# A two-layer graph kernel: three dense chunks of layer 0 in place of four

## The chip, the core and the metric

The kernel runs on one core of a Trainium2 chip, in float32. The metric is the device time of one execution in microseconds. A core has TensorE (PE; PEld is its weight load), VectorE (DVE), ScalarE (ACT), GpSimd (POOL) and SyncE (SP), each with its own instruction stream in order, and 16 DMA engines which serve the transfers that SP, ACT and POOL issue.

## What is computed

```python
x, adj                      # (8, 2048, 128), (2048, 2048); adj = R is sparse, about 0.4%
def L0(inputs, relation):   # layer 0
    sj, si = inputs @ w_j, inputs @ w_i
    res = si[:, :, None] + sj[:, None, :] + relation[None] * w_r + g_b
    return jnp.einsum('bij,bjd->bid', res, inputs) @ weight + bias
def L1(X, A1, A2):          # layer 1, called with A1 = A2 = adj
    x1 = einsum('bnf,nw->bwf', X, A);  x2 = 2 * einsum('bnf,nw->bwf', x1, A) - X
    return relu(concat(X, x1, x2, x1, x2) @ Theta1 + bias)
x = layernorm(x + L0(x, adj))
x = layernorm(x + L1(x, adj, adj))
```

So layer 0 is R times Y, with Y = x times (w_r weight), and terms of rank one; layer 1 is two products with R transposed ("hops").

## The kernel before, in words

The 2048 nodes are 16 chunks of 128. A tile `Y[c]` holds 128 nodes x 8 batches x 128 features (512 KB). R is sparse, so most chunks of output are not computed with all of R: for each chunk the kernel makes seven lists of at most 128 rows each (four lists of 32 output columns, two of 64, one of 128; "tile", "half" and "chunk" lists), gathers those rows of Y from DRAM with seven indirect DMAs of 512 KB, gathers the weights of R that belong to them, and multiplies the gathered rows by small blocks of weights (`listed_rows`), with the diagonal block apart (`own_rows`).

The stages, in the order of the program:

1. *Load stage* (`mask_rows`, `y_chunk`, in one loop over the chunks). R is loaded by rows, each chunk is reduced to a mask of its non-zero tiles of 32 on VectorE, transposed on TensorE, and, if the chunk will be computed by lists, its transpose is stored in the DRAM tensor `rr_d[c]` (L292). x is loaded, and Y made of it. The transposes of the first three chunks (`NA = 3`) stay in SBUF (`first_at`, in `wide[0]` to `wide[2]`), and chunk 0 of layer 0 is summed here already (L342).
2. *Dense stage* (the loop over `c in range(ND)`, `ND = 4`). Chunks 0 to 3 of layer 0 are made with all of R: pass c sums chunk c + 1 over 16 values of j, two products of 128 x 128 by 128 x 512 each (L845). The transposes of chunk 3 are made in the pass before it, from a second load of R (`ar2`, `transpose_group`). Between the products of chosen j stand the steps that make the lists: `tile_ranks`, `tile_lists`, `tile_lists_end`, `half_ranks`, `chunk_ranks`, `candidates` (all with TensorE and VectorE) and eight times `list_round` (VectorE alone: L562 finds the eight largest, L564 takes them out). Here SyncE also issues `copy_r` (R's columns, copied in DRAM to the second half of `rr_d`, L414), `more_rows` (nine more rows of each `rr_d`, L600) and the stores of Y to `y0_d` (L798). GpSimd issues the gathers of weights (`gathers`), each held back until the product of the j before it is done.
3. *List stage of layer 0*: twelve chunks in the order `seq` (9 to 14, 4 to 8, 15). `put(c)` issues what is left of a chunk's weight gathers and calls `keep_r`, by which VectorE masks the gathered weights; `fetch_lists` issues the seven gathers of Y into a ring of nine tiles (`G`, that is `Y[0]` to `Y[8]`); `listed_rows` multiplies (L886); `finish0` adds x and normalizes; `make_u` transposes the result (X1^T, kept in `x1t[c]`) and stores U = X1 times Theta.
4. *First hop* and *second hop* over all 16 chunks with lists, gathering rows of U and of the first hop's result. The four dense chunks' X1^T come back from the DRAM tensor `xt_d`; those of the twelve others have stayed in SBUF (`x1t`).

Weight gathers are a list of jobs `(c, q, n)`: q true for the four tile lists of chunk c, false for the other three. A job of a listed chunk fetches 128 rows of 1 KB from `rr_d` (weights for layer 0 and layer 1 together), one of a dense chunk rows of 512 bytes from R itself. Four slots of `stage` take a chunk's set; at most three sets wait for `keep_r`:

```python
jobs = [(c, q, n) for cs in (seq, range(ND)) for q in (True, False) for c in cs
        for n in range(4 if q else 3)]
...
            if n == 0:
                if len(waiting) == 3:
                    keep_r(*waiting.pop(0))
```

The framework adds the waits between engines and to some extent orders independent instructions; `keep_in_program_order` holds marked ones in the order of the program on their engine, `behind` puts one instruction after another by hand. On every engine and queue the resulting order is fixed when the kernel is built. "Issue" of a DMA by SP, ACT or POOL means that the instruction occupies that stream until it is sent.

Of the kernel before, what the change touches and what calls it, by code (L numbers as in the profile page):

```python
# [18 lines left out]
def kernel(  # L19
# [42 lines left out]
    ND = 4  # L62
# [222 lines left out]
    NA = 3  # L285
# [11 lines left out]
    def mask_rows(n, c):  # L297
# [9 lines left out]
        if c < NA:  # L307
            first_at[c] = transpose_rows(c, a, False, by_chunk(wide[c]))
# [39 lines left out]

    chunks = list(range(NA)) + list(range(ND, NC)) + list(range(NA, ND))
    for n, c in enumerate(chunks):  # L350
        mask_rows(n, c)
        if n == NA - 1:
            xw = wide[3].rearrange("p (n b f) -> p n b f", n=2, b=B)
            xslot += [xw[:, 0], xw[:, 1]]
# [100 lines left out]
    cand = by_chunk(wide[1])  # L455
# [175 lines left out]
    def chunk_lists_end():  # L631
# [6 lines left out]
        nc.tensor.matmul(pn, ones[:, 0:1], miss, start=True, stop=True)  # L638
        nc.vector.tensor_reduce(miss[0:1, 0:1], pn, AX.X, ALU.max)
        return nc.vector.tensor_scalar(  # L640
# [28 lines left out]
    def keep_r(c, q, m, st):  # L669
# [16 lines left out]
    jobs = [  # L686
        (c, q, n) for cs in (seq, range(ND)) for q in (True, False) for c in cs
        for n in range(4 if q else 3)
    ]
# [56 lines left out]
    for n in range(4):  # L746
        pair = wide[n].rearrange("p (n b f) -> p n b f", n=2, b=B)
        spare += [pair[:, 0], pair[:, 1]]
    spare += Y[NG4 + 3:]
# [3 lines left out]
    free = [rc2[:, 4 * N - n * BD:4 * N - (n - 1) * BD].rearrange("p (b f) -> p b f", b=B)  # L753
            for n in range(1, 3)]
    held = {(0, c): Y[c] for c in seq if c >= NG4}
    held |= {(1, c): t for c, t in zip(seq[-2:], free)}
    held |= {(2, c): t for c, t in zip(hops[-7:], [own_t[4], free[0]] + [
# [27 lines left out]
    with nc.allow_non_contiguous_dma(reason="512-byte rows of blocks"):  # L785
        pending, accs, xr = None, acc0, load_x(0, "xr", nc.sync)
        at1, ar2 = first_at[1], None
        for c in range(ND):
            if c + 1 < ND:
                if NA <= c + 2 < ND:  # L790
                    ar2 = load_rows(c + 2, wide[3])
                xr1 = load_x(c + 1, "xr", nc.sync)
            if c < 2:
                copy_r(2 + 5 * c, 7 + 5 * c)
            if 1 <= c <= 2:
                for n in range(8 * c - 8, 8 * c):
                    tc.keep_in_program_order(
                        nc.sync.dma_start(out=y0_d[n * P:(n + 1) * P, :], in_=flat(Y[n]))  # L798
                    )
            if c == 0:  # L800
                make_ub()
                more_rows()
                rank1(0, accs, si_t(0))
            else:
                z = finish0(c, accs, xr, c > 2)
# [277 lines left out]
```

## Time and profile before

| | |
|---|---|
| median of 3 runs | 846.56 us (841.54 to 848.09) |
| the profiled execution | 877.11 us, its span 875.3 us |
| busy, share of the span | PE 89%, PEld 45%, DVE 41%, ACT 20%, POOL 48% |
| DMA | 264.28 MB, mean 302 GB/s |
| load stage, about | 0 to 147 us |
| dense stage, about | 147 to 302 us |
| list stage of layer 0, about | 302 to 475 us |
| first hop, about | 475 to 690 us |
| second hop, about | 690 to 875 us |

The profile is of one execution. A line of the groups gives source line, engine, operation, output and input names with buffer numbers left out, shapes, count, then busy time, the mean of one in ns, and the idle time of the engine just before with what ended it. A line of the timeline gives start and duration in microseconds, engine, source line, operation, names and count, and in brackets the idle time before it with its releaser. Where a releaser is "issue", the profile shows nothing that the engine waited for; "remote" is a releaser that it can't name. Both the DRAM tensors y0_d and y_d appear as y_d. SPq and the like are the queues by which an engine issues DMAs.

### The profile page before, as it was taken

Reading aid. Unit: us, or ns where it says so; the run is one execution under the profiler, and the core shown is the slowest. Engines: PE = TensorE matmul, PEld = TensorE weight load, DVE = VectorE, ACT = ScalarE, POOL = GpSimd, SP = SyncE. Lnnn points to the kernel's source line nnn. Section 1 sums busy time; section 2 is a strip of 40 time slices with the busy share of each in tenths; the row PEclk is TensorE's granted clock in tenths of the full one; section 3 lists DMA queues with packets and bytes.
Section 4 is the critical chain, followed back from the end, with each engine's and each line's share of the span. In section 5 each row is a group of like instructions: output and inputs, shape, how many; then the busy total and the mean of one; then the engine's idle time right before and its main releaser. Section 6 shows DMA issues by size and latency. Waiting matters only on the chain.

```text
span 875.3 us, 10807 instructions
## 1 busy us (share of the span) xinstructions
PE 780.9 (89%) x3631; PEld 393.3 (45%) x3631; DVE 360.5 (41%) x1056; ACT 176.1 (20%) x429; POOL 421.2 (48%) x431
## 2 busy tenths in 40 slices
PE   5999988999997799878986899888999999999994
PEld 4666664455443443333334433333433444545441
DVE  5555665344972364435353000000100045556656
ACT  3655653001111222121212000000000001111111
POOL 0000000015676376766666366666655646666660
PEclk9999999899998699999998899999999999999998
DMA  8699999895383899999997699998999889999994
GB/s 276 205 303 301 276 292 278 237 338 223 88 344 99 310 328 313 335 350 354 338 367 259 236 319 364 311 342 321 377 385 358 286 298 369 352 347 345 346 335 170
DMA packets 172283, 264.28 MB, mean 302 GB/s; under 512 B 17458, under 2 KB 123226, under 8 KB 170044
## 3 DMA queue, kind: packets, MB, share of 16 engines
q0 software_dynamic: 49280, 147.41, 47.4%
q1 hardware_dynamic: 99610, 88.37, 31.7%
q10 hardware_dynamic: 23330, 27.73, 8.8%
q8 instruction: 31, 0.51, 0.2%
q14 instruction: 32, 0.26, 0.1%
HBM read 242.03 MB, written 60.96 MB: 346 GB/s over the span
## 4 chain that ended last, share of the span: by engine, by line
PE 56%; DMA 21%; issue 10%; DVE 5%; ACT 3%; POOL 2%; another core or an unknown queue 2%; SPq 0%; POOLq 0%; DVEq 0%; ACTq 0%
PE acc L886 22%; DMA Y<-y_d,idx 10%; DMA Y<-u_d,idx 7%; PE acc L870 7%; PE acc L944 5%; PE acc L845 4%; PE acc L342 3%; PE acc L332 3%; PE pp L403 2%; POOL Y L647 2%; DVE rc L562 2%; PE pt_a L184 1%; DMA rr_d<-rct 1%; DMA rc<-in_adj_dram 1%
## 5 line engine op out<-in xcount | busy, mean ns | idle before, releaser
L647 POOL DMA_INDIRECT Y<-y_d,idx x196 | 194.8, 994 | 126.3 <-PE acc L886 69.3
L886 PE MATMUL acc<-Y,rc 128*32 128x512 f32 (+2 forms) x896 | 226.4, 610 | 19.6 <-issue 9.7
L647 POOL DMA_INDIRECT stage<-rr_d,idx x84 | 85.5, 1018 | 227.2 <-PE acc L845 200.3
L647 POOL DMA_INDIRECT Y<-u_d,idx x112 | 111.3, 994 | 67.4 <-PE acc L886 35.6
L886 PEld LDWEIGHTS acc<-Y,rc 128*32 128x32 f32 (+2 forms) x896 | 60.9, 128 | 174.9 <-issue 115.8
L886 PE MATMUL acc<-Y,rct 128*32 128x512 f32 (+2 forms) x336 | 96.6, 605 | 19.8 <-issue 10.7
L845 PE MATMUL acc<-Y,wide 128*128 128x512 f32 x192 | 86.9, 602 | 0.5 <-issue 0.5
L870 PE MATMUL acc<-Y,rd 128*128 128x512 f32 x140 | 69.0, 615 | 1.1 <-issue 1.1
L886 PEld LDWEIGHTS acc<-Y,rct 128*32 128x32 f32 (+2 forms) x336 | 23.9, 127 | 83.6 <-issue 58.2
L176 DVE COPY z<-acc 128x512 f32<-128x512 f32 x9 | 6.2, 692 | 122.2 <-PE acc L870 42.9
L845 PEld LDWEIGHTS acc<-Y,wide 128*128 128x128 f32 x192 | 35.9, 194 | 39.9 <-issue 39.9
L219 ACT ACTIVATE st<-st,epst 128x8 f32<-128x8 f32 x32 | 10.0, 311 | 213.9 <-DVE st L220 76.9
L384 DVE TENSOR_TENSOR xs<-acc,xs 128x512 f32<-128x512 f32 x24 | 16.4, 683 | 84.0 <-PE acc L886 50.7
L303 DVE TENSOR_REDUCE rc<-rc 128x64 f32<-128x2048 f32 x16 | 36.5, 2282 | 15.5 <-DMA rc<-in_adj_dram 15.5
L184 PE MATMUL pt_a<-ident,rc 128*128 128x128 f32 x240 | 35.2, 282 | 8.0 <-DMA rc<-in_adj_dram 6.0
L332 PE MATMUL acc<-wx,tr_x 128*128 128x130 f32 x256 | 37.4, 290 | 3.9 <-ACT tr_x L178 3.1
L964 DVE SCALAR_TENSOR_TENSOR z<-z,pt_r 128x512 f32<-128x512 f32 x32 | 20.5, 684 | 47.8 <-PE acc L886 21.3
L332 PEld LDWEIGHTS acc<-wx,tr_x 128*128 128x128 f32 x256 | 33.7, 199 | 14.0 <-ACT tr_x L178 6.4
L342 PE MATMUL acc<-Y,wide 128*128 128x512 f32 x64 | 36.1, 646 | 2.5 <-ACT si L340 1.8
L944 PEld LDWEIGHTS acc<-th,wide 128*128 128x128 f32 x256 | 32.5, 196 | 11.5 <-issue 11.3
L184 PEld LDWEIGHTS pt_a<-ident,rc 128*128 128x128 f32 x240 | 28.8, 145 | 17.6 <-issue 14.3
L944 PE MATMUL acc<-th,wide 128*128 128x128 f32 x256 | 32.7, 280 | 4.1 <-issue 4.1
(210 smaller groups left out, 907.3 us busy)
## 6 DMA issues: line engine op xcount, KB each, us to landing
rc<-in_adj_dram SPq DMA_DIRECT2D x16, 1024.0 KB
rr_d<-rct SPq DMA_DIRECT2D x12, 1024.0 KB
rr_d<-in_adj_dram SPq DMA_DIRECT2D x12, 1024.0 KB
xs<-in_x_dram SPq DMA_DIRECT2D x20, 512.0 KB
y_d<-Y SPq DMA_DIRECT2D x16, 512.0 KB
out_dram<-z ACTq DMA_DIRECT2D x16, 512.0 KB
u_d<-u ACTq DMA_DIRECT2D x14, 512.0 KB
Y<-y_d SPq DMA_DIRECT2D x14, 512.0 KB
```

The lines of the kernel that those rows point to most:

```text
L184: mm = nc.tensor.transpose(pt[:, i, :], s, ident)
L303: nc.vector.tensor_reduce(mk[:, c, :], a.rearrange("p (w f) -> p w f", f=TW), AX.X, ALU.max, apply_absolute_value=True,)
L332: nc.tensor.matmul(py[:, i, 0:D + 2], xt[b // HB][:, (b + i) % HB, :], wx, start=True, stop=True,)
L342: nc.tensor.matmul(acc0[h], first_at[0][:, c, :], Y[c][:, h * HB:(h + 1) * HB, :], start=(c == 0), stop=False, skip_group_check=True,)
L403: mm = nc.tensor.matmul(pp[:, i, :], xt[:, h * HB + i, :], th[:, 0, :], start=True, stop=True)
L562: tc.keep_in_program_order(nc.vector.max(top, part))
L647: g = nc.gpsimd.indirect_dma_start(out=out, out_offset=None, in_=src, in_offset=bass.IndirectOffsetOnAxis(ap=ids[:, n:n + 1], axis=0), bou ...
L845: mm = nc.tensor.matmul(accs1[h], at1[:, j, :], Y[j][:, h * HB:(h + 1) * HB, :], start=(j == 0), stop=False, skip_group_check=True,)
L870: in_order(nc.tensor.matmul(accs[h], r, t[:, h * HB:(h + 1) * HB, :], start=start, stop=stop, skip_group_check=True,))
L886: in_order(nc.tensor.matmul(accs[h][w * t:w * t + w], r[:, o + w * t:o + w * t + w], gs[t][:, h * HB * D:(h + 1) * HB * D], start=False, s ...
L944: in_order(nc.tensor.matmul(accs[h][:, b, :], x1t[c][:, h * HB + b, :], th[:, i, :], start=(b == 0), stop=False, skip_group_check=True,))
L964: nc.vector.scalar_tensor_tensor(z[:, hs, :], z[:, hs, :], 0.0, pt, op0=ALU.max, op1=ALU.add)
```

## The change

`ND` is 3 in place of 4. Chunk 3 goes through the lists like the others: in the load stage its transposes are made and stored with those of the rest, in the list stage it is a thirteenth chunk, and its X1^T stays in SBUF. The dense stage has two passes in place of three. The steps that make the lists stand at other j: `tile_ranks` before the first pass, the tile, half and chunk lists' ranks and the candidates in the first pass, the first two rounds of `list_round` at its end, and the other six in the first half of the second pass. The pass's products from j = 8 on are put behind the last step of the lists (`made`). SyncE issues all eleven remaining copies of R in one row and then, after `more_rows`, all sixteen stores of Y. The weight gathers start at j = 4 and take another order: ten tile sets, and then tile and other sets mixed; 47 stand in the dense stage (58 before).

```diff
-    ND = 4
+    ND = 3
@@ load stage @@
-    NA = 3
-        if c < NA:
+        if c < ND:
             first_at[c] = transpose_rows(c, a, False, by_chunk(wide[c]))
-    chunks = list(range(NA)) + list(range(ND, NC)) + list(range(NA, ND))
-    for n, c in enumerate(chunks):
-        mask_rows(n, c)
-        if n == NA - 1:
+    for n in range(NC):
+        mask_rows(n, n)
+        if n == ND - 1:
@@ lists @@
-    cand = by_chunk(wide[1])
+    cand = by_chunk(wide[3])
-        nc.tensor.matmul(pn, ones[:, 0:1], miss, start=True, stop=True)
+        made = nc.tensor.matmul(pn, ones[:, 0:1], miss, start=True, stop=True)
-    jobs = [
-        (c, q, n) for cs in (seq, range(ND)) for q in (True, False) for c in cs
-        for n in range(4 if q else 3)
-    ]
+    sets = [(c, True) for c in seq[:10]]
+    for n, c in enumerate(seq):
+        sets.append((c, False))
+        if n in (0, 4, 7):
+            sets.append((seq[10 + (0, 4, 7).index(n)], True))
+    sets += [(c, q) for q in (True, False) for c in range(ND)]
+    jobs = [(c, q, n) for c, q in sets for n in range(4 if q else 3)]
@@ places of X1^T and of U @@
-    spare += Y[NG4 + 3:]
+    spare += Y[NG4 + 3:LAST] + [free[0], Y[LAST]]
-    held |= {(1, c): t for c, t in zip(seq[-2:], free)}
-    held |= {(2, c): t for c, t in zip(hops[-7:], [own_t[4], free[0]] + [
+    held[1, LAST] = free[1]
+    held |= {(2, c): t for c, t in zip(hops[-7:], own_t[ND:] + [
@@ dense stage @@
-        at1, ar2 = first_at[1], None
-                if NA <= c + 2 < ND:
-                    ar2 = load_rows(c + 2, wide[3])
-            if c < 2:
-                copy_r(2 + 5 * c, 7 + 5 * c)
-            if 1 <= c <= 2:
-                for n in range(8 * c - 8, 8 * c):
-                    (store of Y[n] to y0_d)
             if c == 0:
+                copy_r(2, NC - ND)
+                tile_ranks()
                 make_ub()
                 more_rows()
                 rank1(0, accs, si_t(0))
             else:
-                z = finish0(c, accs, xr, c > 2)
+                z = finish0(c, accs, xr, c > 1)
+            if c == 1:
+                for n in range(NC):
+                    (store of Y[n] to y0_d)
                 for j in range(NC):
                     if c == 0:
-                        if j == 4:  tile_ranks()
-                        if j == 7:  tile_lists()
-                        if j == 10: at = tile_lists_end(); half_ranks()
-                        if j == 14: chunk_ranks(); z = finish0(c, accs, xr, False); layernorm(z, "0_0", at)
-                    if c == 1 and j < 2: candidates(2 * j); candidates(2 * j + 1)
-                    if c == 1 and (j > 1 and j % 2 == 0 or j == NC - 1):
-                        list_round(j // 2 - (j < NC - 1))
-                    if c == 2:
-                        if j == 6: at = chunk_lists_end(); layernorm(z1, "0_1", at)
-                        if j == 9: layernorm(z, "0_2", at)
-                        if j == 8: fetch_own(0, y0_d, seq[0]); late0 = fetch_block(0, seq[0])
-                    if (c > 0 or j > 11) and not (c == 2 and j > 11):
-                        gathers(1 if j % 4 == 3 else 2, mm)
-                    if c == 2 and j > 11: fetch_lists(0, y0_d, seq[0], 2 * j - 22)
-                    if ar2 is not None and j % 2 == 0 and j >= 8: (transpose_group)
+                        if j == 0:  tile_lists(); z = finish0(c, accs, xr, False)
+                        if j == 3:  at = tile_lists_end(); half_ranks()
+                        if j == 6:  chunk_ranks()
+                        if j in (8, 9): candidates(2 * j - 16); candidates(2 * j - 15)
+                        if j == 10 or j == 13: list_round(j // 13)
+                        if j == 11: layernorm(z, "0_0", at)
+                    else:
+                        if j < 8 and j % 3 < 2: list_round(2 + j // 3 * 2 + j % 3)
+                        if j == 8: made, at = chunk_lists_end(); layernorm(z, "0_1", at)
+                                   fetch_own(0, y0_d, seq[0]); late0 = fetch_block(0, seq[0])
+                    if (c > 0 or j > 3) and not (c == 1 and j > 12):
+                        gathers(3 if c == 1 and j == 12 else 1 if j % 4 == 3 else 2, mm)
+                    if c == 1 and j > 12: fetch_lists(0, y0_d, seq[0], 2 * j - 24)
                     for h in range(2):
                         mm = nc.tensor.matmul(accs1[h], at1[:, j, :], Y[j][...], ...)
+                        if c == 1 and j == 8: behind(mm, made)
                 rank1(c + 1, accs1, sit)
-                if c == 1: gathers(2, mm)
-                if c == 2: fetch_lists(0, y0_d, seq[1], NG4 - 7)
+                if c == 0: gathers(2, mm)
+                else: fetch_lists(0, y0_d, seq[0], 7); fetch_lists(0, y0_d, seq[1], NG4 - 7)
             if pending is not None:
-                make_u(*pending)
+                make_u(*pending, tie=in_order)
@@ hops @@
-                if i == 1 and c == 0:
+                if i == 1 and n == NC - 5:
                     while waiting: keep_r(*waiting.pop(0))
```

In this diff some statements of a branch are drawn together on one line. `in_order` puts TensorE's products one behind the other; it stands ahead of the dense stage now.

## The prediction

> **What bounds the kernel now.** I read the busy shares first, then the chain that ended last, then the groups, then GpSimd's timeline, and last those of SyncE, VectorE and TensorE in the dense stage. TensorE is busy 89% and leads the chain, but its share averages over stages, so I looked for the engine that sets the pace in each.
>
> ```profile
> L647 POOL DMA_INDIRECT Y<-y_d,idx x196 | 194.8, 994 | 126.3 <-PE acc L886 69.3
> L647 POOL DMA_INDIRECT stage<-rr_d,idx x84 | 85.5, 1018 | 227.2 <-PE acc L845 200.3
> L647 POOL DMA_INDIRECT stage<-in_adj_dram,idr x28 | 28.1, 1003 | 12.9 <-issue 8.3 <-DMA Y<-y_d,idx 4.3 <-DMA stage<-in_adj_dram,idr 0.3
> ```
>
> GpSimd issues 420 gathers: these 308 and 112 of U (L647). Its own timeline, one chunk of layer 0:
>
> ```profile
> 347.49 0.99 POOL L647 DMA_INDIRECT Y<-y_d,idx  x1 [2.04 <-PE acc L886]
> 348.78 0.99 POOL L647 DMA_INDIRECT Y<-y_d,idx  x1 [0.31 <-issue]
> ...
> 353.97 1.10 POOL L647 DMA_INDIRECT stage<-rr_d,idx  x1 [0.30 <-issue]
> ...
> 359.29 0.99 POOL L647 DMA_INDIRECT Y<-y_d,idx  x1 [0.30 <-issue]
> 362.28 0.99 POOL L647 DMA_INDIRECT Y<-y_d,idx  x1 [1.99 <-remote]
> ```
>
> Ten gathers, 1.30 us from start to start, then 2 us until TensorE frees a buffer: 362.28 - 347.49 = 14.8 us. Steps with nine gathers (first hop, 523.2 to 536.3) take 13.2 us, steps with seven (602.1 to 612.5) 10.4. The difference is 1.3 us a gather, of Y or of a 64 or 128 KB list of R alike: from 302 us on, the number of gathers is the clock. The dense stage before it (147 to 302) is TensorE's, and ends badly:
>
> ```profile
> 273.35 1.98 PE L375 MATMUL acc<-ub,sit 9*128 9x512 f32 x4
> ...
> 286.61 0.69 DVE L384 TENSOR_TENSOR xr<-acc,xr 128x512 f32<-128x512 f32 x1 [9.97 <-remote]
> ...
> 290.24 2.08 PE L403 MATMUL pp<-th,xt 128*128 128x128 f32 x8 [9.14 <-issue]
> ...
> 304.39 0.99 POOL L647 DMA_INDIRECT Y<-y_d,idx  x1 [12.47 <-PE acc L886]
> ```
>
> The last dense chunk is summed at 275.3; VectorE then sits for 9.97 us on something the profile calls "remote", TensorE for 9.14, GpSimd for 12.47.
>
> **What the skill says.** "Perfetto Trace Analysis", DMA Instruction: for a DMA from GpSimd the profiled end is the end of writing descriptors, not of moving data. The trace agrees: 0.99 us each, while the chain has 6 to 7.5 us for such a gather to land. So 1.30 us is a price of issue, the same for small and large ones. "DMA: Bandwidth & Descriptors", Queues, rings and completion order: on each DMA engine the transfers of one issuing queue are taken up in order; so rows sent behind eleven copies wait for them. Agrees in kind: SyncE is held 3.1 us per copy (15.51 for five). "TensorE: Matmul & The Clock Gate", Part 1: after an idle window of about 3.4 us the clock halves. The windows view agrees: granted 0.50 from 280 to 295. "Runtime: NRT & Kernel Launch", Instruction fetch mechanics: engines stream their instructions through a DMA queue, mostly hidden. The page shows such queues (q8, q14); that the 9.97 us is a fetch I can't show.
>
> **Load stage.** Chunk 3 gets 16 transposes (16 x 0.14 = 2.3 us), four evictions (4 x 0.59), one reduction (2.28) and a 1 MB store. TensorE is busy 15.6 of the 20 us from 120 on and takes it nearly in its gaps: +1.5 us. The store stands before the copies on SyncE and waits for the last evictions: copies begin at 138.3 for 134.1, +4.2. R's second load of chunk 3 (1 MB, L791) goes.
>
> **Dense stage, when gathers can start.** They read rr_d, whose last nine rows (`more_rows`, 13 stores now) stand on SyncE behind all eleven copies, no longer behind five:
>
> ```profile
> 147.00 15.51 SPq L414 DMA_DIRECT2D rr_d<-in_adj_dram  x5
> 162.60 2.51 SPq L592 DMA_DIRECT2D y_d<-ub  x1
> 165.22 6.79 SPq L600 DMA_DIRECT2D rr_d<-sit_all  x12
> ```
>
> 151.2 (147 + 4.2) + 11 x 3.15 + 2.5 + about 4 to land = 192.5: first gather at about 193, as before (192.4, there paced by TensorE at j = 12). It is asked for at j = 4 but can't start. Sixteen stores of Y0 follow from 196 at 1.45 us (11.65 / 8) to 2.4 us (18.90 / 8): done by 235, needed at 256.
>
> **Dense stage, TensorE.** Away: one pass over R, a third of L845's 86.9 us = 29.0, and what went with it: 4 `transpose_group` (2.4), 2.0 of rank-one products. First pass: 58.4 us before (146.9 to 205.3), + 3.7 for `candidates`, + 1.5 for tighter waits, from 148.5: ends at 212. Second pass, eight j of 1.74: 226. There `made` holds it until the lists are ready.
>
> **Dense stage, VectorE.** A list round is MAX8 2.28 + replace 2.27, eight of them with one replace fewer: 34.2 us; each `keep_r` 0.56. `candidates` end 14 us before the first pass does, so round 0 runs 198 to 203. In the built order behind it: keep 0, round 1, keeps 1 and 2, the add of xr1, then rounds 2 to 7 with keeps 3 to 5. Keep 2 needs gather 12, issued at 193 + 11 x 1.3 = 207 and landed 4 to 6 us after its issue ends (6.1 at 253.7 before, Y0 being stored): 212 to 214. Then 1.4 + five rounds 22.9 + 2.3 + three keeps 1.7 = 28.3. The lists end at 241 to 244; I take 242.5. So TensorE idles some 16 us, restarts at 243.3 at half clock (+1.7, counted in the 3 us of waits), does eight more j (14) and the rank-one product (2), then two `make_u` and two block pairs (9.7 + 3 of waits): first listed product (L886 before, L881 after) at 272, for 302.2.
>
> **GpSimd up to there.** 47 gathers for 58 are placed here. The first 39 are issued by 243; the three lists of a chunk need the lists' end, and the last three of the 47 the products of j = 11, at 252: the 47th ends at 256. Nine of Y (11.7): 267.6. Six of R (7.8): 275.4. Y0 to Y4 are free by then: the second chunk's five begin at 275.4 for 304.4: **-29.0 us**. Some 12 of these are the stall at 276 to 290, which nothing in the new order repeats at this place.
>
> **List stage.** After those five: before, 70 of Y and 26 of R; after, 77 and 38. 19 more x 1.3 = 24.7, + one more wait of 1.8, - 3 as two steps carry seven gathers of R, long enough to hide their wait: **+23.5 us**. Bounds: nothing hidden, 26.5; if R's gathers ran in the idle of the ring, 15. TensorE (12 to 13 us of 14.8 busy per step) and DMA (share 0.95 to 1.02) have no room for less than a step per chunk.
>
> **Hops.** 21 dense lists for 28; ten are still issued at the end of layer 0, beside TensorE's own work, so nothing there. In the first hop 11 for 14: 3 x 1.3 = **-3.9 us**. One fetch of `xt_d` less, one of U for chunk 8 more (no longer held): 0. `hop(2)`: 0. The waiting `keep_r` stay at the twelfth chunk.
>
> **Sum.** -29.0 + 23.5 - 3.9 = -9.4 us. Against the profiled execution, 877.1 (span 875.3), that is 867.7, ratio 0.9893; on the median of 846.56: **837.5 us**. Ordinary runs lie 30 us under the profiled one, and I can't say in which stage; that is the first doubt.
>
> **Rivals.** *The stall is the profile's own* (0.22): engines stop together at 276 to 279 (GpSimd by 2.27, TensorE by 1.17), which looks like the recorder; without it the old kernel reaches its five gathers 12 us earlier, and the change is -17.0 + 23.5 - 3.9 = +2.6: 849. Against: the 0.5 clock after it is real. *The ring hides* (0.14): +15 in the list stage for 23.5, 829. For: a 2 us wait in every step. Against: 14.8, 13.2, 10.4 by count. *Late copies* (0.19), the slower side: eleven copies at 4.97 us, the slowest of the page's twelve, and not 3.15 put the first gather at 213; keep 2 and all rounds stand behind it on VectorE, TensorE behind `made`, so 20 us pass through: +10.6, 857. It decides from a first gather later than 202.4. Against: ten of twelve took 3.1 to 3.2. That chunk 3 isn't listed is excluded: the built order shows 91 gathers of Y0.
>
> **Numbers.** Forecast 0.45, own range 829 to 846: its part faster by over 1% (under 838.1) is 0.27. About 1% is what three runs of this kernel tell from no change (841.5 to 848.1). Faster 0.27 + 0.13 (ring) = 0.40; same 0.17 + 0.17 (stall) + 0.01 (ring) + 0.02 (copies) = 0.37; slower 0.01 + 0.05 (stall) + 0.17 (copies) = 0.23. Range 820 to 858: it holds the centres of all four cases.
>
> **What would show it.** First gather near 193 and lists' cast at 243; TensorE idle 14 to 18 us in the second pass; first listed product near 272; steps of 14.8 us and two near 18; last gather of Y0 near 447 (452 before). A first gather after 202.4, or VectorE waiting long in keep 0 to 2, is the late-copies case; equal steps of 14.8 with seven lists of R in them, the ring. A list stage that starts 30 us earlier in the profile with equal medians would make the stall the recorder's, and my sum wrong.

## The result, and the profile after

The changed kernel takes 856.75 us (median of four runs, 854.73 to 859.30) where the kernel before takes 847.33 (841.54 to 848.59): ratio 1.013, 95% interval 1.0081 to 1.0178. It is slower by some 9 to 11 us; the forecast was 837.5. In three later sets of runs every kernel, the one before too, took some 30 us more (before: 880.47, 879.27 and 878.88 in place of 846), and the one profiled execution on which the prediction was built (877.11) was of this longer kind, so that *short* and *long* name the two below and only like is compared with like.

In a long set the changed kernel gives 887.50 against 878.88, ratio 1.0126 (1.0040 to 1.0213): again 1.3%.

The profiled execution after has a span of 857.5 us, a short one. Its dense stage, TensorE first (start, duration, engine, line, names, and in brackets the idle time before it):

```profile
209.35 13.90 PE L846 MATMUL acc<-Y,wide 128*128 128x512 f32 x32
243.12 0.61 PE L608 MATMUL pl<-ident,rc 96*64 96x32 f32 x8 [19.87 <-DVE rc L561]
243.81 16.55 PE L846 MATMUL acc<-Y,wide 128*128 128x512 f32 x32
...
273.62 4.18 PE L881 MATMUL acc<-Y,rct 128*32 128x512 f32 x24
```

The second pass runs its first eight j to 223.2 and then sits for 19.87 us until the list rounds of VectorE (L561) are over. The wait costs a little more than itself: the granted clock is 0.50 up to 247 us and 1.00 only from 251 us on, and the 32 products behind the wait take 16.55 us where the 32 ahead of it took 13.90. The first listed product comes at 273.62. SyncE in the same stage, and VectorE's first list round (L561) and its first three `keep_r` (L674; keep 0, 1 and 2 below):

```profile
147.95 37.80 SPq L413 DMA_DIRECT2D rr_d<-in_adj_dram  x11
185.85 1.97 SPq L591 DMA_DIRECT2D y_d<-ub  x1
187.93 7.07 SPq L599 DMA_DIRECT2D rr_d<-sit_all  x13
```

```profile
196.03 2.29 DVE L561 MAX8 rc<-wide 96x8 f32<-96x2048 f32 x1 [6.42 <-ACT wide L178]
203.35 0.29 DVE L674 TENSOR_TENSOR rct<-stage,has 128x128 f32<-128x128 f32 x1 [2.65 <-DMA y_d<-Y]
209.08 0.29 DVE L674 TENSOR_TENSOR rct<-stage,has 128x128 f32<-128x128 f32 x1 [0.65 <-DMA stage<-rr_d,idx]
214.69 0.29 DVE L674 TENSOR_TENSOR rct<-stage,has 128x128 f32<-128x128 f32 x1 [5.12 <-DMA stage<-rr_d,idx]
```

The rows of `more_rows` stand behind eleven copies, so the first gather of weights is issued at 192.56. Keep 0 to 2 wait 2.65, 0.65 and 5.12 us, 8.4 in all, and the remaining list rounds stand behind them. They wait for their gathers, though the view names a store of Y for the first: each starts 5.7 to 6.7 us after the fourth gather of its set was issued. GpSimd in the list stage, one chunk:

```profile
292.23 1.07 POOL L646 DMA_INDIRECT Y<-y_d,idx  x1 [0.30 <-PE pp L402]
...
301.38 1.01 POOL L646 DMA_INDIRECT stage<-rr_d,idx  x1 [0.30 <-DVE st L215]
...
305.37 1.00 POOL L646 DMA_INDIRECT Y<-y_d,idx  x1 [0.30 <-issue]
```

Ten gathers in 305.37 - 292.23 = 13.1 us: the 2 us wait for a buffer, which the prediction's profile had in every step, is gone. In a short execution of the kernel before it is mostly gone as well: its steps take 12.6 to 14.6 us, but for the last, which has one wait of 7.6 us.

The first of the second chunk's five gathers of Y, in a short execution of the kernel before, in the short one after, and in a long one after:

```profile
290.36 0.98 POOL L647 DMA_INDIRECT Y<-y_d,idx  x1 [6.14 <-PE acc L886]
```

```profile
281.49 0.99 POOL L646 DMA_INDIRECT Y<-y_d,idx  x1 [1.72 <-PE pt_p L184]
```

```profile
290.40 0.99 POOL L646 DMA_INDIRECT Y<-y_d,idx  x1 [6.61 <-PE acc L881]
```

Both kernels, by marks of GpSimd's timeline (second chunk's first five gathers of Y; last gather of Y0; first gather of U; first gather of the first hop's result; end), in us:

| stretch | before, long | after, long | change | before, short | after, short | change | predicted |
|---|---|---|---|---|---|---|---|
| start of the second chunk's five | 304.4 | 290.4 | -14.0 | 290.4 | 281.5 | -8.9 | -29.0 |
| from there to the last gather of Y0 | 147.6 | 174.7 | +27.1 | 143.8 | 159.0 | +15.2 | +23.5 |
| to the first gather of U | 24.0 | 24.0 | 0 | 22.5 | 24.4 | +1.9 | 0 |
| first hop | 204.0 | 201.2 | -2.8 | 190.0 | 192.3 | +2.3 | -3.9 |
| second hop | 195.3 | 195.9 | +0.6 | 197.2 | 200.3 | +3.1 | 0 |
| span | 875.3 | 886.2 | +10.9 | 843.9 | 857.5 | +13.6 | -9.4 |

(Before, long: the first profile. After, long: after4. Before, short: before_again. After, short: the profile above.) The first row failed in both kinds, and by 15 to 20 us.

### The profile page after: what moved, and what is told of

Same layout as the page of the kernel before. It is cut to its first block, busy times and chain, and to the rows that moved or that the text cites. A ratio compares the mean times of both kernels' runs of the same rounds, so it can differ in the third digit from the quotient of the medians.

```text
span 857.5 us, 10765 instructions
## 1 busy us (share of the span) xinstructions
PE 757.0 (88%) x3594; PEld 377.8 (44%) x3594; DVE 363.6 (42%) x1060; ACT 173.7 (20%) x428; POOL 427.3 (50%) x438
## 4 chain that ended last, share of the span: by engine, by line
DMA 39%; PE 21%; issue 7%; POOL 3%; DVE 1%; POOLq 0%; ACT 0%; DVEq 0%
DMA Y<-y_d,idx 22%; DMA Y<-u_d,idx 15%; PE acc L881 12%; PE acc L865 4%; PE acc L939 3%; POOL Y L646 2%; DMA stage<-rr_d,idx 2%; POOL stage L646 1%; PE pt_p L184 1%; PE pt_r L957 1%; PE pp L402 1%; DMA rd<-in_adj_dram 1%; POOLq L646 0%; DVE st L211 0%; DVE z L229 0%
## 5 line engine op out<-in xcount | busy, mean ns | idle before, releaser
L646 POOL DMA_INDIRECT Y<-y_d,idx x203 | 201.4, 992 | 105.7 <-PE acc L881 53.7
L881 PE MATMUL acc<-Y,rc 128*32 128x512 f32 (+2 forms) x896 | 219.8, 605 | 24.5 <-DMA Y<-u_d,idx 14.3
L646 POOL DMA_INDIRECT stage<-rr_d,idx x91 | 92.3, 1014 | 225.5 <-PE pc L554 190.5
L881 PEld LDWEIGHTS acc<-Y,rc 128*32 128x32 f32 (+2 forms) x896 | 58.6, 128 | 175.4 <-issue 83.7
L881 PE MATMUL acc<-Y,rct 128*32 128x512 f32 (+2 forms) x364 | 108.6, 618 | 17.0 <-DMA Y<-y_d,idx 16.2
L846 PE MATMUL acc<-Y,wide 128*128 128x512 f32 x128 | 61.5, 633 | 0.0
L184 PE MATMUL pt_a<-ident,rc 128*128 128x128 f32 x256 | 38.3, 285 | 6.5 <-DMA rc<-in_adj_dram 6.0
L958 DVE TENSOR_TENSOR z<-acc,b1bc 128x512 f32<-128x512 f32 x32 | 21.5, 685 | 42.8 <-PE acc L865 27.6
L311 DVE TENSOR_REDUCE stage<-rct 128x64 f32<-128x2048 f32 x13 | 29.7, 2286 | 23.0 <-ACT rct L178 23.0
L332 PEld LDWEIGHTS acc<-wx,tr_x 128*128 128x128 f32 x256 | 32.8, 194 | 13.8 <-ACT tr_x L178 6.2
L184 PEld LDWEIGHTS pt_a<-ident,rc 128*128 128x128 f32 x256 | 31.4, 147 | 16.3 <-issue 14.8
L342 PE MATMUL acc<-Y,wide 128*128 128x512 f32 x64 | 36.4, 652 | 1.7 <-ACT Y L336 0.9
L846 PEld LDWEIGHTS acc<-Y,wide 128*128 128x128 f32 x128 | 25.0, 203 | 29.0 <-issue 28.1
L959 DVE SCALAR_TENSOR_TENSOR z<-z,pt_r 128x512 f32<-128x512 f32 x32 | 20.5, 682 | 37.9 <-PE pt_r L957 37.9
```

The costliest lines, as they stand in the source:

```text
L184: mm = nc.tensor.transpose(pt[:, i, :], s, ident)
L311: nc.vector.tensor_reduce(mkt[:, :, 4 * c:4 * c + 4], at.rearrange("p j (t f) -> p j t f", f=TW), AX.X, ALU.max, apply_absolute_value=True,)
L332: nc.tensor.matmul(py[:, i, 0:D + 2], xt[b // HB][:, (b + i) % HB, :], wx, start=True, stop=True,)
L342: nc.tensor.matmul(acc0[h], first_at[0][:, c, :], Y[c][:, h * HB:(h + 1) * HB, :], start=(c == 0), stop=False, skip_group_check=True,)
L646: g = nc.gpsimd.indirect_dma_start(out=out, out_offset=None, in_=src, in_offset=bass.IndirectOffsetOnAxis(ap=ids[:, n:n + 1], axis=0), bou ...
L846: mm = nc.tensor.matmul(accs1[h], at1[:, j, :], Y[j][:, h * HB:(h + 1) * HB, :], start=(j == 0), stop=False, skip_group_check=True,)
```

## Experiments

### Which of before's times are its own: before_again, after_again2, after4

The kernel before, unchanged, profiled again.

> The kernel before, unchanged, profiled a second time. Theory A (the first profiled execution of before, span 875.3, held about 28 us that ordinary executions do not have): span 838 to 850; VectorE's 9.97 us and TensorE's 9.14 us of idle between 276 and 290 are gone, the second listed chunk's five gathers of Y begin near 290 instead of 304.4. Theory B (the stall belongs to this kernel and the time is lost under the profiler alone, all over): span 870 to 878 again, with the same idle at 276 to 290. If A, the surplus is either at that one place (then 12 us of it) or also in the list stage and hops: the steps of 14.8 us tell which.

Measured: 845.64 us, span 843.9: theory A. TensorE at the end of its dense stage:

```profile
250.17 0.41 PE L609 MATMUL pl<-ident,rc 96*64 96x32 f32 x8
250.51 0.20 PE L638 MATMUL pn<-miss,ones 128*1 128x16 f32 x2
250.64 17.43 PE L845 MATMUL acc<-Y,wide 128*128 128x512 f32 x40
268.01 1.98 PE L375 MATMUL acc<-ub,sit 9*128 9x512 f32 x4
...
278.82 1.05 PE L886 MATMUL acc<-Y,rct 128*32 128x512 f32 x2
```

No standstill: TensorE goes from the lists' last step (250.17) through the rest of its pass to the first listed product at 278.82 without an idle stretch, and the five gathers begin at 290.36. So 14.0 of the first profile's 31.4 us lay before the list stage, 3.8 in it, 1.5 behind it, and 14.0 in the first hop, less 1.9 in the second.

The changed kernel, unchanged, in two of the long sets:

> The changed kernel profiled a second time, for the spread of one execution: span 852 to 858. If the first hop again takes 191 to 193 us and the second 198 to 200, against 190 and 197 in the kernel before, the hops are a little longer by the change; if they fall on the old values, the difference was the execution's.

> The changed kernel, unchanged. Where the kernel before takes about 847: ratio 1.013 again, list stage 159 us, list stage's start 281.5. Where it takes about 880: about 1.009, list stage 175 us, start 290.

Measured: after_again2 888.65 us (span 886.9, a long execution, so that its 852 to 858 was missed), after4 887.50 (ratio above, where about 1.009 was expected; start at 290.4 and list stage of 174.7 us as expected). Here the changed kernel has the standstill, too, and at the same point of the program, the end of the last dense chunk. after_again2, TensorE, VectorE and ScalarE:

```profile
266.95 1.04 PE L184 MATMUL pt_p<-ident,xr 128*128 128x128 f32 x8
280.08 2.04 PE L402 MATMUL pp<-th,xt 128*128 128x128 f32 x8 [12.09 <-ACT st L219]
```

```profile
279.25 0.69 DVE L176 COPY xt<-pt_p 128x512 f32<-128x512 f32 x1 [12.25 <-remote]
```

```profile
276.32 0.59 ACT L407 COPY u<-pp 128x512 f32<-128x512 f32 x1 [11.06 <-remote]
```

Three engines stand still from some 267 to 276 or 280 and name each other, or nothing, while GpSimd goes on issuing up to 276. In after4 VectorE stands for 10.23 us at this place. The kind of an execution can be read from TensorE's waits (us in total, times, longest). The first profile of before, before_again, after (short) and after4:

```profile
PE acc L886 <- issue: 20.5, 28, 1.8
```

```profile
PE acc L886 <- DMA Y<-y_d,idx: 21.5, 29, 3.8
PE acc L886 <- DMA Y<-u_d,idx: 14.1, 26, 1.3
```

```profile
PE acc L881 <- DMA Y<-y_d,idx: 25.9, 32, 2.3
PE pl L608 <- DVE rc L561: 19.9, 1, 19.9
```

```profile
PE acc L881 <- issue: 22.8, 33, 2.2
PE pl L608 <- DVE rc L561: 19.7, 1, 19.7
```

In the long executions the listed products wait 20.5 and 22.8 us for "issue", nothing that the profile shows; in the short ones that releaser is not among the listed products' leading waits at all. The changed kernel's wait for the lists is there in both kinds (19.9 short; 19.7 and, in after_again2, 23.0 long). What makes an execution long wasn't settled. It isn't the recorder, since the 39 timed executions of the kernel before in the set of after4 took 869 to 884 us; nor is it the chip alone, since the chip of the short set of early_lists also ran two of the three long sets.

### What is the clock of the list stage: more_before, more_after, half_rows, half_width, fewer_r

Clock stands here for what sets the pace. One more gather per listed chunk, 64 KB into a tile that nobody reads:

```diff
             gather(gs[-1], src, idx, n, src.shape[0])
+            if i == 0 and n >= LF:
+                gather(dump, adj128, idr, n, N * NC)
```

> The kernel before with one more GpSimd gather per listed chunk of layer 0: 128 rows of 512 bytes of R into a tile that nobody reads, behind the chunk's seventh gather of Y; twelve more in all, 64 KB each (0.8 MB together, 2.3 us at 340 GB/s). Theory count (GpSimd's number of gathers is the clock of the list stage, as my prediction had it): + 12 x 1.3 = +15.6 us. Theory ring or DMA (the 2 us wait in each step is for a buffer or for bytes, and takes a gather more for nothing): 0 to +3 us.

> The changed kernel with the same extra gather per listed chunk of layer 0, thirteen in all (0.85 MB). In its profile GpSimd issues from 282 to 440 us almost without a wait, so theory count: + 13 x 1.3 = +16.9 us over the changed kernel (about 1.033 against before). Theory DMA (the transfers, at a share of 0.95 to 1.03, set the pace, and issuing merely keeps up): 0 to +4 us (about 1.013 to 1.018 against before).

Measured: more_before 858.35 against 845.43, ratio 1.0123 (1.0070 to 1.0176), so 12.9 / 12 = 1.08 us a gather. more_after 870.82, ratio 1.0267 (1.0211 to 1.0323), 14.1 over the 856.75 of the changed kernel, 14.1 / 13 = 1.08; its list stage is 174.1 us for 159.0, 15.1 for the eleven extra gathers that fall in it. So in the changed kernel the count is a clock. In the kernel before it is one only in part: the list stage grew by 7.9 us (151.7 for 143.8) for ten extra gathers, and GpSimd's waits there, counted over the 0.30 between two gathers, fell from 13.3 to 8.1. more_before, from one extra gather to the next:

```profile
326.58 1.00 POOL L647 DMA_INDIRECT dump<-in_adj_dram,idr  x1 [0.30 <-issue]
...
340.94 1.01 POOL L647 DMA_INDIRECT dump<-in_adj_dram,idr  x1 [0.30 <-issue]
```

Eleven gathers in 14.36 us, 1.305 each.

Then bytes without count. half_rows fetches 64 of the 128 rows of each gather of Y0, half_width rows of half the length into all partitions:

```diff
-            gather(gs[-1], src, idx, n, src.shape[0])
+            gather(gs[-1][0:64], src, idx[0:64], n, src.shape[0])           # half_rows, i == 0
+            gather(gs[-1][:, 0:BD // 2], src.rearrange("n (h f) -> (n h) f", h=2), idx, n,
+                   src.shape[0])                                            # half_width, i == 0
```

> The changed kernel, but the gathers of Y0 in the list stage of layer 0 fetch 64 of their 128 rows; the other 64 rows of each tile keep what was there, so layer 0's sums are not those of the reference. The count of gathers is unchanged (91), the bytes fall by 91 x 256 KB = 23.9 MB. Theory count: the list stage's steps stay 13.0 us and longer, 0 to -5 us in all. Theory DMA (bytes at about 345 GB/s set the pace of the list stage): up to -69 us, bounded by GpSimd's 10 x 1.30 = 13.0 us and TensorE's 12 us in a step; if both limits lie together at 13 us, 0 to -10 us with DMA shares falling to about 0.7.

> The changed kernel, but the gathers of Y0 in the list stage of layer 0 fetch rows of 2 KB instead of 4 KB into all 128 partitions (the wrong rows, and half of each tile keeps what was there): same count of gathers, 23.9 MB less. In the run with 64 of 128 rows the DMA share stayed at 1.01 to 1.07 with 225 GB/s, so those half gathers cost the DMA engines as much as whole ones. Theory count: the list stage's length (159.0 us from the second chunk's five gathers to the last gather of Y0) stays within 5 us, with the DMA share near 0.65. Theory DMA: it shrinks to where TensorE's 12 us a step or less binds, by 12 us or more.

And count nearly without bytes, fewer_r:

```diff
+            if c >= ND and not q and n > 0:
+                continue
             gather_r(*waiting[-1], n)
```

> The changed kernel without two of the three gathers of half and chunk weights of each listed chunk (24 gathers of 128 KB fewer in the list stage, 2 fewer before it; the weights of those lists are then not those of R): bytes fall by 3.4 MB. Theory count: list stage -24 x 1.3 = -31 us until TensorE's 12 us a step binds, so near -12 us (147 for 159.0), plus -2.6 ahead of it: near 843. Theory DMA or TensorE already binding: 0 to -4 us in the list stage.

The windows view from 330 to 360 us, for after, half_rows, half_width and fewer_r (busy us and counts of each engine, then granted clock, DMA share, GB/s):

```profile
330.00:360.00 30.00, 28.04 (x112) 11.46 (x112) 11.99 (x50) 4.45 (x11) 21.76 (x22) 0.94 0.95 346
```

```profile
330.00:360.00 30.00, 24.20 (x85) 7.89 (x85) 9.70 (x39) 4.74 (x11) 19.47 (x21) 0.94 1.07 232
```

```profile
330.00:360.00 30.00, 27.78 (x129) 12.07 (x122) 13.76 (x56) 6.22 (x14) 23.00 (x24) 0.96 0.78 259
```

```profile
330.00:360.00 30.00, 26.12 (x124) 11.51 (x124) 13.76 (x56) 6.22 (x14) 19.17 (x20) 0.89 1.01 376
```

- half_rows: 867.45 us (855.38 to 872.67; the profile is of the longest of the four), against 854.73 to 859.30 with all rows. With half the bytes of Y0 none of the four went below the shortest of those, and in the profile the DMA share is 1.07. It tested neither theory, since half the rows cost the DMA engines no less.
- half_width: 843.87, ratio 0.9960 (0.9941 to 0.9978). The DMA share falls to 0.78, and the list stage is 156.6 us for 159.0; GpSimd issues its 119 gathers of this stage one behind the other, without a wait beyond the usual 0.30. With bytes to spare the count holds it. Of the 13 us off the total, 8.0 lie behind the list stage (16.4 us for 24.4 to the first gather of U), where GpSimd waits for gathers to land.
- fewer_r: 845.67, ratio 0.9986 (0.9966 to 1.0006). Twenty gathers fewer in the list stage, and it is 158.3 us for 159.0, but the equal lengths hide a gain. The stage starts 7.1 us earlier (274.4 for 281.5) and loses that at once: TensorE waits for a block of weights (`rd`) whose transfer keeps SyncE for 10.1 us (6.0 in the changed kernel), and GpSimd for TensorE, so that the first step takes 22.6 us for 13.4:

```profile
287.64 3.78 PE L867 MATMUL acc<-Y,rd 128*128 128x512 f32 x4 [8.79 <-DMA rd<-rr_d]
...
297.05 0.99 POOL L646 DMA_INDIRECT Y<-y_d,idx  x1 [12.51 <-PE acc L883]
```

From the second step to the last gather of Y0 it is 135.7 us for 145.6, 10.0 less. Eighteen gathers are missing there, which by count alone would be 18 x 1.305 = 23.5 us; GpSimd waits 16.9 us (3.5 in the changed kernel), and DMA is at a share of 1.00 and 362 GB/s. TensorE waits 11.7 us for gathered rows, so it isn't the limit there. With the count to spare the bytes hold the stage. So the stage ends 7.8 us earlier, and the first hop is 5.1 shorter (187.2 for 192.3).

So both limits lie close together. For the changed kernel from the second step on, count gives 109 x 1.305 = 142.2 us of the 145.6 measured, and DMA's share is 0.98 over the same stretch. Lowering the bytes alone gives 2 us; leaving out gathers, which carried bytes too, gives less than half of their count.

### What sets the start of the list stage: rows_first, early_lists

rows_first issues `more_rows` ahead of the eleven copies:

```diff
-                copy_r(2, NC - ND)
                 tile_ranks()
                 make_ub()
                 more_rows()
+                copy_r(2, NC - ND)
```

> The changed kernel with the nine more rows of each rr_d (more_rows, and what it needs) issued on SyncE ahead of the eleven copies of R instead of behind them. Theory path (VectorE's 8.4 us of waits in keep 0, 1 and 2 stand in front of the list rounds, the rounds in front of TensorE's second pass, and the second pass in front of the list stage): first gather near 175 instead of 192.6, no wait in keep 0 to 2, lists' end near 235 instead of 243, first listed product near 265 instead of 273.6, and 6 to 9 us off the time, near 849. Theory clock (GpSimd's count after 247 is all that matters): the same first gather near 175, but the list stage starts no earlier, 0 to -3 us.

Measured: 849.07, ratio 1.0015 (0.9988 to 1.0041), 7.7 us under the changed kernel. It went as theory path has it: first gather 173.0, no wait in keep 0 to 2, and

```profile
236.12 0.61 PE L608 MATMUL pl<-ident,rc 96*64 96x32 f32 x8 [13.54 <-DVE rc L561]
...
266.04 4.22 PE L881 MATMUL acc<-Y,rct 128*32 128x512 f32 x24
```

The lists end 7.0 us earlier (236.12 for 243.12), the first listed product comes 7.6 earlier, the five gathers begin 8.1 earlier (273.4), and the list stage keeps its length (160.1).

early_lists puts the whole chain at the head of the first pass:

```diff
-                copy_r(2, NC - ND)
+                copy_r(2, 6)
                 tile_ranks()
+                tile_lists()
+                half_ranks()
                 make_ub()
                 more_rows()
+                copy_r(6, NC - ND)
...
+                        if j == 1:
+                            at = tile_lists_end()
+                            chunk_ranks()
+                        if j in (2, 3):
+                            candidates(2 * j - 4)
+                            candidates(2 * j - 3)
+                        if j in (4, 6, 9, 11, 14):
+                            list_round((4, 6, 9, 11, 14).index(j))
...
+                        if j in (0, 3, 5):
+                            list_round(5 + (0, 3, 5).index(j))
```

> The changed kernel with the whole chain that makes the lists at the head of the first dense pass (tile lists, half and chunk ranks, candidates by j = 3, list rounds from j = 4 on), four copies of R, then more_rows, then the other seven. Theory path plus clock: rounds start near 178 instead of 196, first gather near 175 instead of 192.6, lists' end near 220, TensorE's 19.9 us wait in the second pass gone, first listed product near 254 instead of 273.6; GpSimd then issues the same number of gathers from 20 us earlier: about 838, 1% under the kernel before. Rival: DMA (share 0.95 to 1.03 from 273 on) can't take the same bytes in less time, or the copies and stores of Y0 now collide with the gathers: the list stage gets longer by as much as it starts earlier, 850 to 857.

Measured: 842.34, ratio 0.9937 (0.9907 to 0.9967): it beats both kernels, the one before by 0.6%. TensorE's waits:

```profile
PE acc L881 <- DMA Y<-y_d,idx: 28.6, 36, 3.3
...
PE pl L608 <- DVE rc L561: 6.5, 1, 6.5
```

The wait for the lists falls from 19.9 to 6.5 us, the five gathers begin at 267.8 (281.5), the list stage is 159.3. The rounds began at 190 and not at 178 as expected, since TensorE does `make_ub` between the half and the chunk ranks; 13.7 us of the expected 20 came.

The same kernel beside the changed one, in a long set:

> The changed kernel with the list chain at the head of the first pass, a second time, beside the changed kernel itself. Where the kernel before takes about 847: 0.6% less than it, as in the first run. Where it takes about 880: if lists bind there too, 10 to 15 us less than the changed kernel; if the standstill at the start of the list stage takes it back, as in split_rows3 (1.009), no less than the changed kernel.

Measured: 872.34, ratio 0.9966 (0.9936 to 0.9997), 15.2 us under after4. The standstill is there (15.29 us of TensorE), and doesn't take the gain back.

### Trying for the rest: split_rows, split_more, before_split

split_rows sends the rows of `rr_d`, which need only si, ahead of all copies, and the store of ub behind them:

```diff
-        tc.keep_in_program_order(nc.sync.dma_start(out=y0_d[N:, :], in_=flat(ub)))   # in more_rows
...
-                copy_r(2, NC - ND)
+                more_rows()
+                copy_r(2, NC - ND)
                 tile_ranks()
-                make_ub()
-                more_rows()
-                rank1(0, accs, si_t(0))
+                tile_lists()
+                at = tile_lists_end()
+                half_ranks()
...
+                        if j == 2:
+                            make_ub(); (store of ub); rank1(0, accs, si_t(0)); finish0 of chunk 0
+                        if j in (2, 4, 7, 10, 12, 15):
+                            list_round((2, 4, 7, 10, 12, 15).index(j))
```

split_more adds to this `sets = [(c, q) for q in (True, False) for c in seq]` and 61 gathers in the dense stage; before_split is the same idea with four dense chunks. All of their runs were long ones.

> The same split of more_rows and the same early chain, but the changed kernel's own order of jobs and 47 gathers in the dense stage. Theory path: list stage begins 6 to 8 us earlier than in early_lists and lasts the same 159 us: near 835. If split_more is faster than this by 4 us or more, gathers taken out of the list stage pay; if not, the list stage is bound by bytes and by TensorE by then.

> The changed kernel with more_rows split: the rows of rr_d (they need si alone) go ahead of all copies, the store of ub to y0_d behind them; the list chain stands at the head of the first pass with make_ub and the first chunk's sums behind it; all thirteen tile sets are the first jobs, and 61 gathers in place of 47 stand in the dense stage. Theory path plus clock plus DMA: first gather near 160 (178.6 in early_lists), rounds from 178, lists' end near 216, no wait of TensorE (6.5 us in early_lists), list stage begins 6 to 8 us earlier than there, and holds 14 gathers of 128 KB fewer, of which, both limits being at 13 us a step, the bytes give back some 5 us: near 831. Rival: the fourteen gathers only move GpSimd's load ahead of the first nine gathers of Y0, which then start later; the list stage begins no earlier than in early_lists and the whole is 838 to 842.

> The kernel before (four dense chunks) with the same split of more_rows, the copies in one row, and the list chain at the head of its first pass; weight gathers from j = 4 on, 72 in the dense stage in place of 58. Theory 'lists bind with three chunks, TensorE with four': TensorE's work up to the first listed product is unchanged, so that product stays near 278 us, and only the 14 gathers less in the list stage (1.8 MB, at most 5 us by bytes) and its 7.6 us wait at the end can give anything: 838 to 846. Rival 'lists bind in both': the first listed product comes 15 us or more earlier, and the time falls to 832 or less.

> The same split and early chain with the changed kernel's own order of jobs and 47 gathers in the dense stage. Theory path: list stage begins 6 to 8 us earlier than in early_lists, lasts the same 159 us: near 835. If the two split kernels differ by less than 2 us, gathers moved out of the list stage are worth nothing there.

> The changed kernel with more_rows split (rows of rr_d ahead of all copies, the store of ub behind them), the list chain at the head of the first pass, all thirteen tile sets first among the jobs, 61 gathers in the dense stage. Where the kernel before takes about 847: theory path plus clock plus bytes: first gather near 163, lists' end near 216, list stage 6 to 8 us earlier than in early_lists (267.8) and some 5 us shorter (159.3): near 831. Rival: the fourteen gathers only move GpSimd's load ahead of the first nine gathers of Y0: 838 to 842. Where the kernel before takes about 880, as in the last set, this kernel showed 1.2% more than it, because it then starts its listed chunks later than the changed kernel does.

> Four dense chunks with the same split and early chain, 72 weight gathers in the dense stage. Theory 'lists bind with three chunks, TensorE with four': first listed product near 278 us as in the kernel before, so the gain is only that of the list stage, 838 to 846. Rival 'lists bind in both': first listed product 15 us earlier, 832 or less.

> The split and early chain with the changed kernel's own jobs. Where the kernel before takes about 847: list stage 6 to 8 us earlier than in early_lists (267.8), near 835. Where it takes about 880: 1.009 to 1.015 again.

Measured against the kernel before of the same set: split_rows 1.0147 (1.0108 to 1.0185), 1.0090 (1.0058 to 1.0121) and 1.0061 (1.0033 to 1.0090); split_more 1.0118 (1.0044 to 1.0191) and 1.0196 (1.0099 to 1.0293); before_split 1.0053 (1.0017 to 1.0089), and 878.15 against 879.27 without an interval. None beats early_lists, which has 0.9966 in the set of the last split_rows.

In that last run the first gather came at 164 us as meant, but the first list round only at 187.2 (189.6 in early_lists4): VectorE's copies for `make_ub` and the add of chunk 0 had come to stand ahead of it, and the lists' end stayed at 228.5 (227.6). For split_more the rival in its expectation came true in kind: in the set with split_rows2 its second chunk's five begin at 303.9 (289.3), the list stage is 163.7 us (175.4), and nothing is gained.

before_split was to show that with four dense chunks an earlier chain gives nothing, and doesn't show it cleanly. In the first of its runs VectorE was through with its keeps at 229.0 and then stood for 15.33 us, on a releaser that the profile calls "remote", before the lists' last steps (L617 at 244.36, L638 at 245.76), and TensorE waited 14.7 us for L638. In the second run VectorE stood there for 9.55 us and TensorE waited 11.6. That looks like the standstill of the long executions, but in both runs TensorE stands still a second time at the usual place (17.91 us, and 8.94 and 6.29). It fell on the very step in question, so the two runs decide nothing. That TensorE, and not the lists, binds four dense chunks therefore rests on the trace of before_again alone: VectorE's last round ends there at 245.3, and TensorE comes to the lists' cast at 250.17 without a wait. Whether the kernel before would gain from an earlier chain, as the changed one does, is not shown.

## Why the prediction was wrong

It was wrong in direction, by one term of the sum, and that term was wrong for two reasons. In the short executions the start of the list stage is 20.1 us off, the list stage 8.3 us the other way, and the stretches behind it are 11.2 us longer than forecast; in the long ones 15.0, 3.6 and 1.7.

*The failed step: "the second chunk's five begin at 275.4 for 304.4: -29.0 us".* First, of the 304.4, "some 12 are the stall at 276 to 290, which nothing in the new order repeats at this place". It does repeat there: in long executions the changed kernel stands still from some 267 to 280, and its five start at 290.4; in short ones the kernel before doesn't stand still, and its five start at 290.4, too, 14.0 us earlier than in the profile. Either way the difference loses what was counted for the stall. The prediction's rival *the stall is the profile's own* took 12 us off for this and came nearer (849), but with the wrong cause: executions that nobody profiled are just as long.

Second, 275.4 was 6.1 early (281.49). The lists ended as forecast (243.1 for 242.5), the first listed product was 1.6 late (273.6 for 272), the 47th gather ended 2.7 late (258.7 for 256), and GpSimd then waited 0.1, 1.4 and 1.4 us over its 0.30 for slots and buffers that were assumed free. What is left is -8.9: of a whole pass of TensorE (29 us) a standing wait of 19.9 takes most, because the list rounds, which stood beside TensorE's work before, end at 243.0 now and ended at 245.3 in before_again, where TensorE came to them only at 250.2. The prediction had this wait, too (16 us), and it stood in its 275.4.

*Load and dense stage, the rest.* The copies begin at 136.8 (138.3). The first gather came at 192.56 (193), which is luck in part: the last eleven of them began 3.2 us earlier (147.95 for 151.2) and took 3.2 us longer (37.8 for 34.65) than was counted. The first pass ends at 209.3 (212), the eighth j of the second at 223.2 (226), TensorE idles 19.9 us (16). The half clock behind that idle stretch was counted with 1.7 us; it cost 2.65. The rival *late copies* gave 857, the number that came, by luck: it needed a first gather after 202.4. But its other sign, VectorE waiting in keep 0 to 2, is there with 8.4 us, and the path that it named is the one that binds: rows_first takes 7 us out of it, and the kernel gets 7.7 shorter.

*List stage, "+23.5 us".* +15.2 in short executions, +27.1 in long ones, so it sits between two cases of which the prediction knew one. In the long ones the 3 us taken off were not there: the two steps with seven gathers of R take 20.4 us each, not some 18, and keep their wait; the prediction's bound with nothing hidden was 26.5. In short ones the rival *the ring hides* has the number, +15, and a mechanism that fits: nineteen more gathers fill waits of before (13.3 us of waits there, of which 7.3 in one place at the end; 4.0 after). The bytes allow the same number: seven gathers of 512 KB and twelve of 128 KB are 5.2 MB, 14.6 us at the 359 GB/s and the share of 1.00 that DMA shows over this stage in before_again (an estimate). No run tells the two apart. The price of a gather held at the issue (1.30), with 1.08 end to end. The sentence that DMA has "no room for less than a step per chunk" was right, and more than a bound: fewer_r shows bytes as a clock once the count is lowered, half_width the count once the bytes are.

*Hops, "-3.9".* Between -2.8 and +2.3. In the short executions three gathers fewer in the first hop buy nothing: GpSimd waits 26.7 us there before and 32.8 after anyway, most of it for TensorE. The +2.3 wasn't taken apart, nor the +1.9 ahead of it and the second hop's +3.1; the second hop lies between 195.2 and 200.3 over all profiles with 128 rows of Y0, of both kernels.

*The first doubt.* The text said that "ordinary runs lie 30 us under the profiled one, and I can't say in which stage", and scaled the sum by their ratio. The ratio was harmless; what couldn't be scaled is a stall of that execution that stood in the sum as a gain.

## What to carry to other kernels

When a profiled execution is several per cent longer than the timed ones, find its surplus first (waits of products for "issue", several engines still at once, an unnamed releaser), and book none of it as a gain of the change: either kernel may have it or not. Work taken from one engine moves a stage's end only until the next chain is late, so follow what was beside it (here VectorE's rounds behind `keep_r` behind `more_rows`), and move that chain together with the work: early_lists is the same change with the chain moved, and turns 1.3% slower into 0.6% faster. Where a step has two limits at nearly the same height, a test that lowers one shows little; lower each alone to see that there are two, and look at the steps one by one, since a late first step can hide what the others gained (fewer_r).

## What the runs showed of the hardware

- In the one profile of half_rows, indirect gathers of 64 rows into 64 partitions kept the DMA engines as busy as those of 128 rows: share 1.07 at 232 GB/s, against 0.95 at 346. Rows of half the length into all 128 partitions did free them (0.78 at 259), though not by half.
- GpSimd's 1.30 us from gather to gather held for 4 KB, 2 KB, 1 KB and 512-byte rows alike; with 64 rows the instruction itself took 0.93 us in place of 0.99.
- After TensorE had idled for 19.87 us its granted clock was 0.50 for about 4 us and 0.75 in the mean of the next 4, and 32 products took 16.55 us for 13.90.
- In long executions VectorE stood still for 10 to 17 us on "remote" around the step from the dense to the list stage (9.97 us in the first profile, 12.25 in after_again2, 10.23 in after4, 17.29 in early_lists4), TensorE and ScalarE with it for much of that time, and in the two runs of before_split VectorE also did so earlier (15.33 and 9.55). The cause stays open.
